# Gate chains spread over more pieces in a fused recurrence and mixture-of-experts kernel

## The chip, the cores and the metric

The kernel runs on one core of a Trainium2 chip. The metric is the device time of one execution in microseconds (us). The core has five engines that run beside each other, each taking its own instructions in order: the tensor engine (PE) for matrix products, the vector engine (DVE), the scalar engine (ACT), GpSimd (POOL) and SyncE (SP), of which the last here only starts transfers. Engines wait for each other through semaphores. Transfers between device memory and the on-chip memory (SBUF) are issued by SP, ACT and POOL and carried out by 16 DMA engines. Matrix products land in PSUM, a small second memory.

## What is computed

Two layers over x of 4 batches, 1024 time steps and 1024 channels, in 32-bit floats:

```python
x = x + ffn0(cond0(x, f, f, w0, u0, cond))       # f is the side input
x = x + ffn1(cond1(x, f, f, w1, u1, cond))

def cond(r, k, v, w, u, time_emb):
    tf = sigmoid(sum(time_emb))
    decay = exp(-exp(w)) * (0.5 + 0.5 * tf)
    ek = exp(min(k, 30)); ekv = ek * v
    # forward and backward over time: a = a * decay + ekv, b = b * decay + ek
    num = nf + nb - ekv + exp(min(u + k, 30)) * v
    den = df + db - ek + exp(min(u + k, 30))
    return sigmoid(r) * num / max(den, 1e-8) * (0.8 + 0.2 * tf)

def ffn0(c): return einsum(c, weight * scale) + bias

def ffn1(c):
    h = rmsnorm(c) * norm_w
    w, ids = top_4(softmax(h @ router_w.T)); w = w / sum(w)
    routed = sum over the 4 of w * ((silu(h @ w1g[id]) * (h @ w1u[id])) @ w2[id])
    shared = (silu(h @ sg) * (h @ su)) @ sd
    return c + routed + shared
```

All of cond apart from sigmoid(r) depends on f alone, so it can be worked out for both layers before x of the second layer is known. The second layer's sigmoid(x), called the gate here, is multiplied in later.

## The kernel before

**Two phases.** The first phase, up to about 2,100 us, makes everything but the experts: the recurrences, the first product, gate, norm, router and the shared feed-forward. The second phase takes 68 pairs of expert blocks and 12 single ones and is the same in both kernels. The change lies in the first phase alone.

**The mixer** (`mixing`, L232) works out the recurrences in units (batch, tile of 128 channels, layer), on DVE (scans L278 and L290, products L308 to L322), ACT (exponentials, logarithm, sigmoid) and with one accumulating DMA of POOL (L323). Each finished unit goes to device memory (c0_d for the first layer, c1_d for the second; L338) and is loaded back in chunks of 512 time steps. It is a generator: each `yield` gives the DVE time that the step was reckoned to take. For the first batch all eight units of the first layer come before those of the second.

**Pieces.** The work of PE is cut into pieces, mostly eight matrix products of 128x512 that end in one PSUM tile, reckoned at 6.9 us (`W_PIECE`). `order` (L850) lists them and `run` goes through the list. For each piece `run` first calls `early` (the loads) of this piece and of the two after it, then draws mixer steps as long as the reckoned DVE work is below the reckoned PE work, then issues the piece. `mix_until` draws mixer steps without that limit until a unit is made. The follow-up of a piece is put off with `after(n, f)`: f is issued at the end of the piece n places later. All this settles only the order of the instructions in each engine's queue, fixed when the kernel is built; at run time each engine goes as far as its semaphores allow.

**Chunks.** The 4096 tokens are eight chunks of 512 (q, two for each batch). The pieces that the change touches:

- `first_ffn(q, gated)`: the first layer's product, eight pieces (L429). With `gated` (chunks 2 to 7) the residual sum x follows (L434), and then the gate of the tile. For chunks 0 and 1 the gates come later.
- `gate(q, ot, x)`: sigmoid on ACT one piece later, on DVE the product with c1 (L458) and on ACT its square (L459) two pieces later, and three pieces later an accumulating DMA on POOL (L462) and a matrix product of ones with the square (L465), by which the squares of all channels are summed in the PSUM tile `ss`. After the eighth of these the norm begins.
- `late_gate(q)`: the gates of chunks 0 and 1 as eight pieces with little PE work. Each loads c1 and x (L482, L484) in `early`, so two pieces ahead, and waits for the c1 unit there with `mix_until`.
- `norm_route(q)`: a generator that `run` steps once a piece: square root on ACT, reciprocal (L499) and scaling (L502) on DVE, router product (L509) on PE, its copy on ACT (L511), then transposes (L520, L528), top four (L531 to L536), ranks, and 16 scattering DMAs on POOL (L591). After chunk 7 it goes on to `plan` (lists of tokens for each expert) and `first_weights` (loads of the first two units of the second phase, L788 and L795).
- `shared_up(q)`: 16 pieces (L620), in turn the gate and the up product of 128 columns; Silu on ACT a piece after the former, the product of both on DVE (L629) a piece after the latter, or at once for the last. `shared_down(q)`: eight pieces (L648), the sum with the residual (L662), and a turn by PE and ACT (L653, L654).

In `order` the first batch is: `first_ffn(0)`, `first_ffn(1)`, the gates of chunk 0, seven empty pieces, then `shared_up(0)` with a gate of chunk 1 after each second piece, the remaining gates, `shared_down(0)`, `shared_up(1)`, `shared_down(1)`. PSUM tiles of these products (`mm`) have four buffers, sigmoid and square (`y`, `sq`, pool `pch`) two each, x six.

Of the kernel before, what the change touches and what calls it, by code (L numbers as in the profile page):

```python
# [8 lines left out]
FP = mybir.dt.float32  # L9
I32 = mybir.dt.int32  # L10
U32 = mybir.dt.uint32
AF = mybir.ActivationFunctionType
ALU = mybir.AluOpType
# [9 lines left out]
P = 128  # L23
CH = 512
# [7 lines left out]
def kernel(  # L32
# [15 lines left out]
    nc = tc.nc  # L48
# [6 lines left out]
    NC = C // P  # L55
    NI = I // P
    NSI = SI // P
# [25 lines left out]
    ones = const.tile([P, P], FP, name="ones")  # L83
# [106 lines left out]
    def right(name, bufs):  # L190
        return a.enter_context(tc.tile_pool(name=name, bufs=bufs, side="right"))
# [8 lines left out]
    px = right("px", 6)  # L200
    pw0 = right("pw0", 3)
    pch = right("pch", 2)
    psm = right("psm", 1)
    ps_ss = a.enter_context(tc.tile_pool(name="ps_ss", bufs=1, space=PSUM))
    ps_sm = a.enter_context(tc.tile_pool(name="ps_sm", bufs=1, space=PSUM))
# [3 lines left out]
    W_PIECE, W_SMALL = 6.9, 1.0  # L209
# [9 lines left out]
    def other(to, of, func, **kw):  # L219
        table[0] = func  # L220
        nc.scalar.activation(to, of, func, **kw)
# [139 lines left out]
    def after(pieces, f, vector=0.0, tensor=0.0):  # L361

        told[0] += 1
        due.append((count[0] + 1 + pieces, told[0], f, vector, tensor))
# [35 lines left out]
    def first_ffn(q, gated):  # L400

        b, cols = q // NCH, bass.ts(q % NCH, CH)
        c0s, tiles, xs = [], {}, {}

        def early(ot):
            if not gated:

                nc.sync.dma_start(out=resT_d[ot, :, bass.ts(q, CH)], in_=xT[b, bass.ts(ot, P), cols])
            else:
                xs[ot] = px.tile([P, CH], FP, name="x")  # L410
                nc.sync.dma_start(out=xs[ot], in_=xT[b, bass.ts(ot, P), cols])
            if ot == 0:
                mix_until(*((b, ct, 0) for ct in range(NC)))
                if q == 0:
                    work["tensor"] += LATENCY
                for ct in range(NC):
                    c0s.append(pc0.tile([P, CH], FP, name="c0"))
                    nc.sync.dma_start(out=c0s[ct], in_=c0_d[b, ct, :, cols])
            tiles[ot] = pw0.tile([P, NC, P], FP, name="w0t")
            nc.sync.dma_start(out=tiles[ot], in_=w0[ot])  # L420
            if gated:
                mix_until((b, ot, 1))
                c1s[q, ot] = (ph, pc1)[q % NCH].tile([P, CH], FP, name="c1")
                nc.sync.dma_start(out=c1s[q, ot], in_=c1_d[b, ot, :, cols])

        def do(ot):
            mm = ps_mm.tile([P, CH], FP, name="mm")
            for it in range(NC):
                nc.tensor.matmul(mm, lhsT=tiles[ot][:, it, :], rhs=c0s[it], start=(it == 0), stop=(it == NC - 1))  # L429
            to = resT_d[ot, :, bass.ts(q, CH)]  # L430
            scale = v["s0"][:, ot : ot + 1]
            if gated:
                x = xs.pop(ot)
                after(1, lambda: nc.vector.scalar_tensor_tensor(x, mm, scale, x, ALU.mult, ALU.add), W_HALF)  # L434
                after(2, lambda: nc.sync.dma_start(out=to, in_=x))
                gate(q, ot, x)
            else:
                y = px.tile([P, CH], FP, name="x")
                after(1, lambda: nc.scalar.activation(y, mm, AF.Copy, scale=scale))
                after(2, lambda: nc.gpsimd.dma_start(out=to, in_=y, accum_op=ALU.add))  # L440

        return [Piece(lambda ot=ot: do(ot), lambda ot=ot: early(ot)) for ot in range(NC)]

    sums = {}

    def gate(q, ot, x):

        b = q // NCH
        c1 = c1s[q, ot]
        held = {}  # L450

        def sigmoid():
            held["y"] = pch.tile([P, CH], FP, name="y")
            other(held["y"], x, AF.Sigmoid, bias=v["b0"][:, ot : ot + 1])

        def gated():
            held["sq"] = pch.tile([P, CH], FP, name="sq")
            nc.vector.scalar_tensor_tensor(c1, c1, nosc[:, b : b + 1], held["y"], ALU.mult, ALU.mult)  # L458
            nc.scalar.activation(held["sq"], c1, AF.Square)  # L459

        def add():
            nc.gpsimd.dma_start(out=resT_d[ot, :, bass.ts(q, CH)], in_=c1, accum_op=ALU.add)  # L462
            if ot == 0:
                sums[q] = ps_ss.tile([P, CH], FP, name="ss")
            nc.tensor.matmul(sums[q], lhsT=ones, rhs=held["sq"], start=(ot == 0), stop=(ot == NC - 1))  # L465
            if ot == NC - 1:
                beside.append(norm_route(q))

        after(1, sigmoid)
        after(2, gated, W_HALF)  # L470
        after(3, add, 0.0, W_SMALL)

    def late_gate(q):


        b, cols = q // NCH, bass.ts(q % NCH, CH)
        xs = {}

        def early(ot):
            mix_until((b, ot, 1))  # L480
            c1s[q, ot] = (ph, pc1)[q % NCH].tile([P, CH], FP, name="c1")
            nc.sync.dma_start(out=c1s[q, ot], in_=c1_d[b, ot, :, cols])  # L482
            xs[ot] = px.tile([P, CH], FP, name="x")
            nc.sync.dma_start(out=xs[ot], in_=resT_d[ot, :, bass.ts(q, CH)])  # L484

        return [
            Piece(lambda ot=ot: gate(q, ot, xs.pop(ot)), lambda ot=ot: early(ot), tensor=W_SMALL)
            for ot in range(NC)
        ]

    scattered = []
# [1 line left out]
    def norm_route(q):  # L493
# [2 lines left out]
        hs = [c1s[q, ct] for ct in range(NC)]  # L496
        rs = p1.tile([P, CH], FP, name="rs")
        other(rs, sums.pop(q), AF.Sqrt, bias=eps_c, scale=1.0 / C)
        nc.vector.reciprocal(rs, rs)  # L499
        yield 3.4, 0.0  # L500
        for ct in range(NC):
# [106 lines left out]
    def shared_up(q):  # L608
        wts = {}

        def early(f, n):
            wts[f, n] = pw.tile([P, NC, P], FP, name="wpc")
            nc.sync.dma_start(
                out=wts[f, n], in_=(sg, su)[n][:, bass.ts(f, P)].rearrange("(k p) f -> p k f", p=P)
            )

        def do(f, n):
            mm = ps_mm.tile([P, CH], FP, name="mm")
            for kt in range(NC):
                nc.tensor.matmul(  # L620
                    mm, lhsT=wts[f, n][:, kt, :], rhs=c1s[q, kt], start=(kt == 0), stop=(kt == NC - 1)
                )
            if n == 0:
                act = acts[q, f] = pa.tile([P, CH], FP, name="sact")
                after(1, lambda: other(act, mm, AF.Silu))
            else:
                act = acts[q, f]

                after(int(f + 1 < NSI), lambda: nc.vector.tensor_tensor(act, act, mm, ALU.mult), W_HALF)  # L629

        return [
            Piece(lambda f=f, n=n: do(f, n), lambda f=f, n=n: early(f, n)) for f in range(NSI) for n in range(2)
        ]
# [143 lines left out]
    def load(unit, at):  # L777

        kind, n = unit
        e = nc.values_load(  # L780
            have["experts"][0:1, kind, n : n + 1],
            engines=[SP],
            min_val=0,
            max_val=E - 1,
            skip_runtime_bounds_check_because="worked out above from counts, and held to that range",
        )
        for k in range(2):
            nc.sync.dma_start(  # L788
                out=have["w1"][at][k],
                in_=w1[bass.ds(e, 1), k * NK * P : (k + 1) * NK * P].rearrange("e (k p) f -> p (e k) f", p=P),  # L790
            )
            if k == 0:
                yield
        yield
        nc.sync.dma_start(  # L795
            out=have["w2"][at], in_=w2[bass.ds(e, 1)].rearrange("e (k p) f -> p (e k) f", p=P)
        )
        yield
# [51 lines left out]
    def order():  # L850

        pieces = first_ffn(0, False) + first_ffn(1, False) + late_gate(0)

        pieces += [Piece(lambda: None, tensor=2.0) for _ in range(7)]
        up, gates = shared_up(0), late_gate(1)
        for i, piece in enumerate(up):
            pieces.append(piece)
            if i % 2 == 1:
                pieces.append(gates.pop(0))
        pieces += gates  # L860
        pieces += shared_down(0) + shared_up(1) + shared_down(1)
        pieces += first_ffn(2, True) + first_ffn(3, True) + shared_up(2) + shared_down(2) + shared_up(3)
        for b in range(2, B):
            q = NCH * b
            pieces += first_ffn(q, True) + first_ffn(q + 1, True) + shared_down(q - 1)
            pieces += shared_up(q) + shared_down(q)
            if b + 1 < B:
                pieces += shared_up(q + 1)
        return pieces
# [476 lines left out]
```

## Time and profile before

| | |
|---|---|
| median of 3 runs | 5193.74 us (5193.41 to 5196.67) |
| the profiled execution | 5197.78 us, its span 5195.8 us |
| PE busy | 4884.7 us, 94% |
| DVE busy | 3129.8 us, 60% |
| ACT busy | 1433.3 us, 28% |
| POOL busy | 764.6 us, 15% |
| granted clock of PE over the span | 0.989 |
| mean over DMA | 205 GB/s |
| 400 to 500 us: PE, DVE, ACT busy | 84.9, 84.7, 75.2 us |
| 600 to 700 us: PE, DVE, ACT busy | 99.8, 87.8, 67.5 us |
| 1500 to 1800 us: PE, DVE busy | 299.1, 28.7 us |

All views are of one execution, with times from the start of the span. A row of the timeline has its start, its time on the engine, engine, line, operation, result and sources, and in brackets the idle time of the engine before it and what ended that. A product of 32-bit floats stands in the trace as two records, so eight products are x16. Line numbers are those of the kernel before.

### The profile page before, as it was taken

To read this page: it belongs to the slowest core of one execution; us is meant where nothing else is said; L and a number is where in the kernel's file an instruction comes from. 1 tells how busy PE (TensorE), PEld (TensorE's weight loads), DVE (VectorE), ACT (ScalarE), POOL (GpSimd) and SP (SyncE) were. 2 spreads that over 40 slices of the span, in tenths; PEclk is the share of its full clock that TensorE was granted. 3 is DMA by queue.
4 is the path that set the end of the run, shared out by engine and by line. 5 is a ranking of instruction groups with operands and counts; after the bars stand their busy time and mean duration, and the time that the engine had idled before them with its cause. 6 is when DMAs were issued, how large, how long until landed. Compare 5 with 4: busy or idle time off the path is not lost.

```text
span 5195.8 us, 36650 instructions
## 1 busy us (share of the span) xinstructions
PE 4884.7 (94%) x13004; PEld 2258.9 (43%) x13004; DVE 3129.8 (60%) x3280; ACT 1433.3 (28%) x1830; POOL 764.6 (15%) x716
## 2 busy tenths in 40 slices
PE   0478999999999999899999999999999999999999
PEld 0233444444444444444444444444444444444444
DVE  9988898899700221556565656565656556665621
ACT  5557566667500120111111111111111111111110
POOL 0113201300210020111111111111111111111110
PEclk9989999999999999999999999999999999999999
DMA  4676669568733754567777677767676777767684
GB/s 137 201 206 174 170 199 266 162 188 254 206 96 101 214 158 152 196 217 239 216 233 231 222 231 226 231 214 238 211 247 207 242 228 220 234 215 242 216 234 122
DMA packets 517155, 1064.92 MB, mean 205 GB/s; under 512 B 29857, under 2 KB 259362, under 8 KB 516354
## 3 DMA queue, kind: packets, MB, share of 16 engines
q1 hardware_dynamic: 386338, 744.70, 42.4%
q0 software_dynamic: 67600, 210.28, 19.2%
q10 hardware_dynamic: 63024, 107.50, 5.9%
q8 instruction: 105, 1.72, 0.1%
q14 instruction: 88, 0.72, 0.0%
HBM read 844.13 MB, written 203.56 MB: 202 GB/s over the span
## 4 chain that ended last, share of the span: by engine, by line
PE 59%; ACT 0%; DMA 0%; issue 0%; DVE 0%; POOLq 0%; ACTq 0%
PE gA L1072 14%; PE gB L1072 9%; PE gC L1072 9%; PE dA L1072 7%; PE dB L1072 5%; PE dC L1072 4%; PE tr L926 2%; PE gA L960 2%; PE gB L960 2%; PE tr L1009 1%; PE dA L1022 1%; PE dB L1022 1%; PE gC L1257 0%; PE gB L1257 0%; PE dA L1257 0%; PE gA L1257 0%
## 5 line engine op out<-in xcount | busy, mean ns | idle before, releaser
L620 PE MATMUL mm<-c,wpc 128*128 128x512 f32 x1792 | 782.7, 597 | 0.0
L429 PE MATMUL mm<-c,w0t 128*128 128x512 f32 x1024 | 451.6, 597 | 199.7 <-DMA w0t<-in_w 199.7
L620 PEld LDWEIGHTS mm<-c,wpc 128*128 128x128 f32 x1792 | 341.4, 192 | 421.0 <-issue 419.4
L1072 PE MATMUL gA<-w,hsT 128*128 128x512 f32 x1088 | 491.4, 594 | 0.0
L1072 PE MATMUL gB<-t_up,s_up 128*128 128x512 f32 x1088 | 489.1, 592 | 0.0
L1072 PE MATMUL gC<-w,s_up 128*128 128x512 f32 x1088 | 489.1, 592 | 0.0
L1056 POOL DMA_INDIRECT sum_d<-y,tokens x148 | 304.7, 2059 | 919.8 <-DMA sum_d<-y,tokens 541.4
L648 PE MATMUL mm<-sact,wpc 128*128 128x512 f32 x896 | 399.4, 601 | 10.9 <-DVE sact L629 10.9
L911 POOL DMA_INDIRECT hs<-h_d,tokens x148 | 149.6, 1011 | 1635.5 <-PE tr L926 1546.2
L429 PEld LDWEIGHTS mm<-c,w0t 128*128 128x128 f32 x1024 | 195.3, 192 | 446.8 <-issue 437.7
L1072 PEld LDWEIGHTS gC<-w,s_up 128*128 128x128 f32 x1088 | 206.7, 190 | 260.2 <-issue 260.2
L1072 PEld LDWEIGHTS gB<-t_up,s_up 128*128 128x128 f32 x1088 | 206.7, 190 | 260.2 <-issue 244.2
L807 DVE TENSOR_TENSOR t_up<-w,w 128x2048 f32<-128x2048 f32 x136 | 310.7, 2285 | 0.0
L1072 PEld LDWEIGHTS gA<-w,hsT 128*128 128x128 f32 x1088 | 202.3, 191 | 229.1 <-issue 229.1
L290 DVE TENSOR_TENSOR_SCAN fg<-decay,tail,fg 128x1024 f32<-128x1024 f32 x128 | 292.9, 2329 | 0.0
L648 PEld LDWEIGHTS mm<-sact,wpc 128*128 128x128 f32 x896 | 169.4, 193 | 212.4 <-issue 198.5
L1072 PE MATMUL dB<-t_down,s_down 128*128 128x512 f32 x544 | 256.9, 594 | 0.1
L1072 PE MATMUL dA<-w,actT 128*128 128x512 f32 x544 | 255.8, 592 | 0.0
L1072 PE MATMUL dC<-w,s_down 128*128 128x512 f32 x544 | 255.8, 592 | 0.0
L927 ACT COPY hsT<-tr 128x512 f32<-128x512 f32 x296 | 172.7, 588 | 293.3 <-PE tr L926 293.3
L1072 PE MATMUL gA<-t_up,hsT 128*128 128x512 f32 x544 | 244.5, 592 | 0.0
L997 ACT ACTIVATE act<-c 128x512 f32<-128x512 f32 x68 | 42.9, 630 | 708.9 <-DVE c L993 708.9
(238 smaller groups left out, 6211.1 us busy)
## 6 DMA issues: line engine op xcount, KB each, us to landing
w<-in_w SPq DMA_DIRECT2D x240, 2048.0 KB, 9.0
fg<-euk POOLq DMA_DIRECT2D x64, 512.0 KB, 6.3
c_d<-r ACTq DMA_DIRECT2D x64, 512.0 KB, 7.9
c<-c_d SPq DMA_DIRECT2D x128, 256.0 KB, 6.3
w0t<-in_w SPq DMA_DIRECT2D x64, 512.0 KB, 5.9
wpc<-in_sg SPq DMA_DIRECT2D x56, 512.0 KB, 4.0
wpc<-in_su SPq DMA_DIRECT2D x56, 512.0 KB, 3.7
wpc<-in_sd SPq DMA_DIRECT2D x56, 512.0 KB, 5.1
```

Of the source, the lines that this page charges most:

```text
L290: nc.vector.tensor_tensor_scan(fg[:, m, ::-1], decay[L][:, ct, b : b + 1].to_broadcast([P, T]), fg[:, m, ::-1], tail[:, m : m + 1], ALU.mu ...
L429: nc.tensor.matmul(mm, lhsT=tiles[ot][:, it, :], rhs=c0s[it], start=(it == 0), stop=(it == NC - 1))
L620: nc.tensor.matmul(mm, lhsT=wts[f, n][:, kt, :], rhs=c1s[q, kt], start=(kt == 0), stop=(kt == NC - 1))
L648: nc.tensor.matmul(mm, lhsT=wts[ct][:, f, :], rhs=acts[q, f], start=(f == 0), stop=(f == NSI - 1))
L807: nc.vector.tensor_tensor(to, x, y, ALU.subtract)
L911: nc.gpsimd.indirect_dma_start(out=hs, out_offset=None, in_=h_d, in_offset=bass.IndirectOffsetOnAxis(ap=tokens[:, i, self.n : self.n + 1], ...
L926: nc.tensor.transpose(tr[:, r, :], hs[:, bass.ts(4 * q + r, P)], ident)
L927: nc.scalar.copy(self.hsT[:, 4 * q : 4 * q + 4, b, :], tr)
L960: nc.tensor.matmul(ps, lhsT=self.hsT[:, k, 0, :], rhs=w[k // NK][:, k % NK, bass.ts(n, I)], start=(k == 0), stop=(k == NC - 1),)
L1022: nc.tensor.matmul(ps, lhsT=self.actT[:, k, 0, :], rhs=w[:, k, bass.ts(n, 512)], start=(k == 0), stop=(k == NI - 1),)
L1056: nc.gpsimd.indirect_dma_start(out=sum_d, out_offset=bass.IndirectOffsetOnAxis(ap=tokens[:, i, self.n : self.n + 1], axis=0), in_=y, in_of ...
L1072: nc.tensor.matmul(ps, lhsT=x[:, k, :], rhs=w[:, k, :], start=(k == 0 and not more), stop=(k == half - 1), skip_group_check=more,)
```

## The change

The sigmoid's result y gets a pool of its own with four buffers, and the square is written over y. The sum waits one piece longer after the gate's product. With `gated` the whole chain starts a piece later (lag 2). The late gates wait for one unit ahead only, and load within the piece before; a piece that only loads the first comes ahead of them. The norm has one more step between square root and reciprocal. The product with the up part comes two pieces later, not one. Around the last gate of chunk 0 the reckoned PE times of the empty pieces change: one of 4.0 before it, seven of 0.5 behind it instead of 2.0 (LATENCY is 12.0).

```diff
@@ pools
     pch = right("pch", 2)
+    psq = right("psq", 4)
@@ first_ffn
-                gate(q, ot, x)
+                gate(q, ot, x, 2)
@@ gate
-    def gate(q, ot, x):
+    def gate(q, ot, x, lag=1):
...
         def sigmoid():
-            held["y"] = pch.tile([P, CH], FP, name="y")
+            held["y"] = psq.tile([P, CH], FP, name="y")
             other(held["y"], x, AF.Sigmoid, bias=v["b0"][:, ot : ot + 1])
 
         def gated():
-            held["sq"] = pch.tile([P, CH], FP, name="sq")
             nc.vector.scalar_tensor_tensor(c1, c1, nosc[:, b : b + 1], held["y"], ALU.mult, ALU.mult)
-            nc.scalar.activation(held["sq"], c1, AF.Square)
+            nc.scalar.activation(held["y"], c1, AF.Square)
...
-            nc.tensor.matmul(sums[q], lhsT=ones, rhs=held["sq"], start=(ot == 0), stop=(ot == NC - 1))
+            nc.tensor.matmul(sums[q], lhsT=ones, rhs=held["y"], start=(ot == 0), stop=(ot == NC - 1))
...
-        after(1, sigmoid)
-        after(2, gated, W_HALF)
-        after(3, add, 0.0, W_SMALL)
+        after(lag, sigmoid)
+        after(lag + 1, gated, W_HALF)
+        after(lag + 3, add, 0.0, W_SMALL)
@@ late_gate
-        def early(ot):
+        def load(ot):
             mix_until((b, ot, 1))
...
-        return [
-            Piece(lambda ot=ot: gate(q, ot, xs.pop(ot)), lambda ot=ot: early(ot), tensor=W_SMALL)
-            for ot in range(NC)
+        def do(ot):
+            if ot + 1 < NC:
+                load(ot + 1)
+            gate(q, ot, xs.pop(ot))
+
+        return [Piece(lambda: None, lambda: load(0), tensor=0.0)] + [
+            Piece(lambda ot=ot: do(ot), tensor=W_SMALL) for ot in range(NC)
         ]
@@ norm_route
         other(rs, sums.pop(q), AF.Sqrt, bias=eps_c, scale=1.0 / C)
+        yield 0.0, 0.0
         nc.vector.reciprocal(rs, rs)
@@ shared_up
-                after(int(f + 1 < NSI), lambda: nc.vector.tensor_tensor(act, act, mm, ALU.mult), W_HALF)
+                after(2 if f + 1 < NSI else 0, lambda: nc.vector.tensor_tensor(act, act, mm, ALU.mult), W_HALF)
@@ order
         pieces = first_ffn(0, False) + first_ffn(1, False) + late_gate(0)
 
-        pieces += [Piece(lambda: None, tensor=2.0) for _ in range(7)]
+        pieces.insert(-1, Piece(lambda: None, tensor=LATENCY / 3))
+        pieces += [Piece(lambda: None, tensor=0.5) for _ in range(7)]
         up, gates = shared_up(0), late_gate(1)
```

## The prediction

> **What bounds the kernel now.** I read the busy rows first, then what the tensor engine (PE) waited for, its timeline at those waits, and what the vector engine (DVE) waited for at the same moments.
>
> The page's slices: busy tenths, 130 us each.
>
> ```profile
> PE   0478999999999999899999999999999999999999
> DVE  9988898899700221556565656565656556665621
> ```
>
> PE is the bound from 197 us on; DVE is nearly as full until about 1,430 us, while the mixer (the scans) runs. Busy PE is 4884.7 of 5195.8 us, so 311 us are idle. Who was waited for (total, times, longest):
>
> ```profile
> PE mm L429 <- DMA w0t<-in_w: 199.7, 5, 197.2
> PE ss L465 <- ACT sq L459: 54.9, 12, 16.1
> PE mm L648 <- DVE sact L629: 10.9, 2, 9.0
> PE tr L926 <- DMA hs<-h_d,tokens: 10.8, 1, 10.8
> PE tr L520 <- ACT rT L654: 8.5, 6, 7.3
> PE tr L509 <- DVE c L502: 5.0, 1, 5.0
> ```
>
> The first row is the mixer's lead-in, which the change doesn't touch. The target is the second: the one-column-sum matmul that closes each gate (L465) stands in PE's queue before sigmoid, gate and square are through. PE's timeline there (start, us, what, idle before):
>
> ```profile
> 336.89 2.08 PE L465 MATMUL ss<-sq,ones 128*128 128x512 f32 x2 [16.08 <-ACT sq L459]
> ...
> 358.88 8.60 PE L509 MATMUL tr<-c,rw_sb 128*32 128x512 f32 x16 [5.04 <-DVE c L502]
> ...
> 369.45 7.03 PE L620 MATMUL mm<-c,wpc 128*128 128x512 f32 x16
> ...
> 407.67 2.07 PE L465 MATMUL ss<-sq,ones 128*128 128x512 f32 x2 [6.46 <-ACT sq L459]
> 409.54 15.76 PE L620 MATMUL mm<-c,wpc 128*128 128x512 f32 x32
> 425.13 1.02 PE L465 MATMUL ss<-sq,ones 128*128 128x512 f32 x2
> 425.99 13.90 PE L620 MATMUL mm<-c,wpc 128*128 128x512 f32 x32
> ```
>
> A stall costs more than its idle time: after 6.46 us of it the same two blocks took 2.07 and 15.76 us, against 1.02 and 13.90 without one. And DVE's waits in the same stretch:
>
> ```profile
> 389.53 1.23 DVE L256 TENSOR_TENSOR ekv<-ek,k 128x1024 f32<-128x1024 f32 x1 [5.14 <-ACT ek L217]
> ...
> 433.01 1.23 DVE L314 TENSOR_TENSOR r<-r,fg 128x1024 f32<-128x1024 f32 x1 [3.92 <-DMA fg<-euk]
> ...
> 511.99 0.69 DVE L629 TENSOR_TENSOR sact<-sact,mm 128x512 f32<-128x512 f32 x1 [6.49 <-PE mm L620]
> ...
> 1055.99 0.69 DVE L629 TENSOR_TENSOR sact<-sact,mm 128x512 f32<-128x512 f32 x1 [8.09 <-ACT sact L221]
> ```
>
> So the engines wait for each other in turn. DVE executes in order: what it loses, every later gate loses.
>
> **The change part by part.** The operations and their number stay, but for one more table load on ScalarE (ACT). What moves is seen in the order of each engine's instructions, built from both kernels.
>
> *Gates of the first chunk (313 to 359 us).* Only the next unit is awaited before a gate is issued, so on DVE gate 4 comes before the 11.6 us of mixer work (330.04 less 318.48) instead of behind it, and the pair L321/L322 (2.4 us) moves ahead of the norm's reciprocal. Followed row by row: DVE keeps the mixer work up to there; ACT gets gate 4's square and gate 5's sigmoid between two mixer steps and switches tables twice more before the exponential, so the last c1 unit is written later: 2 x 1.28 us, with the sigmoid and square some 2.8 us after overlap. Before, its load went out at 337.6 and its sigmoid ran at 346.0, so most of that delay lies beside other work: sigmoid at 347.5, gate 8 at 348.3 (before: 350.26), reciprocal at 352.5 (354.60). Gain **2.1**, and 0.7 because a matmul block now fills the wait of L528: **2.8**.
>
> Here a rule speaks against the change. The Trainium skill ("ScalarE: Activation LUTs", What ACT_TABLE_LOAD costs) puts a switch at 1283 ns and a drain of about 1380 ns, 2.66 us together, and advises grouping functions by table set; the change splits the groups. The row has the load alone: it starts at 310.97 for 1.28 us, and the sigmoid follows at 312.26. By the page two switches would cost 5.3 us and turn 2.1 into a loss of 0.7; by the row, 2.6. I take the row.
>
> *Gates of the second chunk (372 to 545 us).* Their closing matmul moves from three pieces behind the gate to four, and the gates themselves one up-pair later, because the list of gates now begins with a piece that only loads: the first sum stands behind the seventh up piece, before it was the fourth. That is 20.6 us more cover (3 x 6.87). The four stalls (6.46, 5.02, 3.63, 5.17: 20.3) and the slow blocks after them (4 x 1.05, and 1.86, 2.01, 0.62, 0.87: 9.6) could all go: **29.9**. But DVE must keep up. Its L531 (logits out of PSUM) ran at 370.07 unhindered; now PE has up piece, L509, up piece (8.6 + 6.9 + 6.9) before it issues L528, so DVE, done at about 365.6, waits until 379.6: **14 us new**, with all the gates behind it.
>
> *Four buffers y, the square written into y.* Same space (y and sq had two each). It removes ACT's waits for PE at the square (51.6 us, eight times), which cost nothing themselves.
>
> *The product with the up matmul (L629) two pieces later.* DVE's waits for PE there (6.49, 1.32) go. What it costs: the PSUM tile is held a piece longer, with four of them. Before, the product ended 7.2 to 8.6 us ahead of the next user in the tightest place (1,014 and 1,026 us); a piece later, 0.3 to 1.7 us are left. Between 0 and some 7 us; hidden if DVE gains about what PE gains. Taken as 0.
>
> *Gated chunks (two pieces more to the sum).* Stalls of 1.52, 3.94 and 2.17 us go, with 1.8 us of slow blocks: 7.2 before 1,056 us, 2.2 after; with the wait for w0t of 0.75 at 1,284 us, which followed the stall, about **3** after.
>
> *Up to down (sact).* PE waits 1.88 (720 us) and 8.99 (1,048 us), with 2.5 us of slow matmuls after the second. In the new order the third block's last Silu no longer stands behind a mixer exponential that waited 3.79 us for a DMA.
>
> *The end of the stage (2,046 to 2,112 us).* Sum and reciprocal come three pieces later (lag 1, sum 1, the added yield 1), so plan, token lists and the first expert weights do too: SyncE's queue has the first load behind the fifth down piece instead of the second, 3 x 7.3 = 22 us. The second half of the first unit's w1 still goes where the fourth load went, 2,076; landing takes up to 13.1 us, so 2,090, and its user starts at 2,096: hidden, with 6 us of cover. What can't be hidden: three 2 MB loads now run beside the first token gather, for which PE waits 10.8 us. It took 5.8 us; gathers took 3.9 to 10.2. From 0 to 4.4, and I take **3**.
>
> **The sum.** At 1,056 us there are two accounts. PE, if nothing is ever late: 2.8 + 29.9 + 1.9 + 11.5 + 7.2 = 53. DVE: 6.5 less mixer work issued by then (seven empty pieces of 2.0 become 0.5 each plus one of 4.0), the waits of 5.14, 4.29 and 3.92 (the third follows from the second; POOL's slot writes blocked that DMA for 13 us, now for about 4), 6.49, 1.32 and 8.09 (29.2), and half of three whose order changes (8.7 at the reciprocal, 9.2 at 719 us, 6.2 at a sigmoid: 12); less 14 and about 7 for L531 in the second chunk: 27. The later engine decides, so 27, not 53. With 3 after it and 3 lost at the end: **27 us**. The profiled execution took 5197.78 (span 5195.8), 4 above the median; the difference goes onto the median: 5193.74 - 27 = **5167**.
>
> **The rivals.**
> 1. *DVE's arrears eat it* (chance 0.16): the stalls leave L465 and come back at L629, L509 or as a PSUM wait, and only the 6.5 us of postponed mixer work stay. For: DVE is 89% busy from 600 to 1,200 us. Against: much of its idle time is waiting for PE and ACT. Time 5187.
> 2. *DVE becomes slower than before* (0.12): L531, behind one more PE piece in each norm, waits 14 us in the first and up to 7 in the next three while the mixer runs: 35. If none of the removed waits stays away, 35 - 6.5 = 28 and more than it can hide; with a third of them gone, 5193.7 + 28 - 10 = 5212. It decides from new waits above 6.5 plus what the removed ones give. Against: L531 waited only 1.7 us in the second norm, where pieces already lay between.
> 3. *All of the cover works* (0.14): DVE's own waits go with PE's, two thirds of PE's account: 35 + 3 + 8 for the tr wait at 587 us (7.28) and its slow blocks, nothing lost at the end: 5148.
> That the gates don't move is excluded by the order.
>
> **How the numbers follow.** Forecast 0.58, the rivals 0.16, 0.12 and 0.14. A measurement here can't tell less than 0.2% (10 us) from no change. Faster: 0.58 + 0.14 and a little of the first rival: 0.75; within: 0.14; slower: 0.11. The forecast's own range is 5155 to 5180 (the L629 and gather ends, and the halved waits lost or won); to leave out no more than 2 in 10 it reaches to 5148 and 5190.
>
> **What would show it.** Right: L465 under 15 us in PE's waits, a wait of 10 to 15 us at DVE's L531 near 380 us, the first up matmul at about 357 us, the PE row near 1,048 us less than 3 us idle, the end of the last down piece near 2,067 us. Wrong: PE waiting for L629 at an up matmul, L509 waiting for L502 near 557 us, or a gather above 8 us at the end.

## The result and the profile after

The changed kernel took **5170.45 us** (median of five runs, 5167.34 to 5180.32) against 5195.63 (5193.41 to 5196.67): a ratio of 0.9957 with a 95% interval of 0.9943 to 0.9972, 25 us faster. The profiled execution took 5180.32 us (span 5178.3), the longest of the five, so its views show less of a gain than the median.

Who PE waited for (total, times, longest), changed kernel:

```profile
PE mm L430 <- DMA w0t<-in_w: 202.5, 7, 197.0
PE ss L465 <- ACT y L459: 42.2, 8, 17.2
PE tr L932 <- DMA hs<-h_d,tokens: 17.8, 2, 17.0
...
PE mm L653 <- DVE sact L634: 3.7, 1, 3.7
```

The sums' row fell from 54.9 us only to 42.2, the row from up to down (L629 before, L634 now) from 10.9 to 3.7; the wait at the first token gather grew from 10.8 to 17.8. PE's timeline, changed kernel:

```profile
342.22 2.07 PE L465 MATMUL ss<-y,ones 128*128 128x512 f32 x2 [17.24 <-ACT y L459]
...
358.68 9.45 PE L625 MATMUL mm<-c,wpc 128*128 128x512 f32 x16 [5.00 <-issue]
368.06 7.05 PE L514 MATMUL tr<-c,rw_sb 128*32 128x512 f32 x16
...
444.87 1.66 PE L465 MATMUL ss<-y,ones 128*128 128x512 f32 x2 [4.58 <-ACT y L459]
...
466.62 2.08 PE L465 MATMUL ss<-y,ones 128*128 128x512 f32 x2 [5.20 <-ACT y L459]
...
511.50 2.07 PE L465 MATMUL ss<-y,ones 128*128 128x512 f32 x2 [4.73 <-ACT y L459]
```

In the new order the first up piece goes ahead of the router product (L514), and of the four stalls of the second chunk three are left, 14.5 of 20.3 us. DVE in the same stretch shows the price that was forecast, the wait for the logits (L536), and two waits behind a transfer that landed late:

```profile
382.58 0.29 DVE L536 COPY lg<-small 128x128 f32<-128x128 f32 x1 [14.98 <-PE small L533]
...
443.22 1.23 DVE L315 TENSOR_TENSOR r<-r,fg 128x1024 f32<-128x1024 f32 x1 [4.00 <-DMA fg<-euk]
449.13 1.23 DVE L257 TENSOR_TENSOR ekv<-ek,k 128x1024 f32<-128x1024 f32 x1 [4.68 <-ACT ek L218]
```

Where the gain sits, from the start of the same piece in both timelines (shift against before, us): first down piece of chunk 0 +0.8 (512.6 to 513.4); that of chunk 1 -4.1; first piece of chunk 2 -7.2; first up piece of chunk 3 -19.6 (1110.9 to 1091.3); end of the last down stage -22.2 (2097.0 to 2074.8); first turn of gathered tokens -16.0 (2107.8 to 2091.8).

A second profile of the same kernel (below) belongs to an execution of 5166.32 us. There the shifts are -10.2, -15.2, -18.7, -30.8, -34.6 and -28.7. The median lies between the two.

### The profile page after: what moved, and what is told of

Its sections match the earlier page's. It is cut to its first block, busy times and chain, and to the rows that moved or that the text cites. A ratio compares the mean times of both kernels' runs of the same rounds, so it can differ in the third digit from the quotient of the medians.

```text
span 5178.3 us, 36602 instructions
## 1 busy us (share of the span) xinstructions
PE 4875.7 (94%) x13004; PEld 2256.4 (44%) x13004; DVE 3130.4 (60%) x3280; ACT 1435.0 (28%) x1831; POOL 762.3 (15%) x716
## 4 chain that ended last, share of the span: by engine, by line
PE 87%; DVE 5%; DMA 4%; ACT 3%; issue 2%; POOL 0%; SPq 0%; ACTq 0%; DVEq 0%; POOLq 0%
PE gA L1078 14%; PE mm L625 12%; PE gC L1078 9%; PE gB L1078 9%; PE dA L1078 7%; PE mm L430 7%; PE mm L653 6%; PE dB L1078 5%; PE dC L1078 5%; PE tr L932 2%; PE gA L966 2%; PE gB L966 2%; PE tr L1015 1%; DMA xg<-in_xT 1%; PE tr L514 1%
```

## The experiments

| kernel | median us | ratio to before (95%) |
|---|---|---|
| changed kernel again | 5172.33 | 0.9956 (0.9943 to 0.9970) |
| without the norm's added step | 5188.53 | 0.9988 (0.9979 to 0.9997) |
| old empty pieces | 5186.38 | 0.9985 (0.9976 to 0.9994) |
| sum two pieces behind, not three | 5171.95 | 0.9955 (0.9942 to 0.9969) |
| product with up one piece later | 5173.06 | 0.9951 (0.9937 to 0.9965) |
| lag 1 for chunks 2 to 7 | 5174.04 | 0.9962 (0.9948 to 0.9975) |
| old loading of late gates | 5167.93 | 0.9946 (0.9932 to 0.9959) |
| before, with the later sum alone | 5190.50 | 0.9992 (0.9984 to 1.0001) |
| nine empty pieces | 5164.45 | 0.9936 (0.9923 to 0.9950) |
| last norm three pieces earlier | 5171.88 | 0.9953 (0.9940 to 0.9967) |
| these two together | 5157.73 | 0.9929 (0.9915 to 0.9942) |
| and the old loading | 5154.99 | 0.9923 (0.9909 to 0.9936) |

**1. The changed kernel again**, no edit.

> The changed kernel once more. In its first profile an accumulating transfer of the mixer (fg<-euk, issued at 426.65 us) landed only at 443.1 us and made the vector engine and ScalarE wait some 8 us; in the profile of the kernel with the earlier last norm, which has the same instructions there, it was issued at 425.75 us and nothing waited for it. Theory X (this one landing decides between two courses of the first batch): a profile with the early landing has the first down piece of chunk 0 at about 502 us instead of 513.5 and a span of about 5168 us; the median stays at 5168 to 5172. Rival: the profile is like the first, and the 5 to 10 us between executions come from elsewhere (the end).

The first down piece of chunk 0 began at 502.4 us, as theory X has it, and the span was 5164.3 us (about 5168 was said; the median of 5172.33 lies at the upper edge of what was said). PE's waits in this stretch:

```profile
457.04 1.12 PE L465 MATMUL ss<-y,ones 128*128 128x512 f32 x2 [0.88 <-ACT y L459]
...
500.57 2.07 PE L465 MATMUL ss<-y,ones 128*128 128x512 f32 x2 [6.23 <-ACT y L459]
```

One kernel so has stalls of 14.5 or 7.1 us here, depending, as far as the two profiles show, on when one transfer lands (last section). The experiments that follow are compared by their medians, and their profiles with this second one.

**2. Without the norm's added step.**

```diff
-        yield 0.0, 0.0
         nc.vector.reciprocal(rs, rs)
```

> The changed kernel without the added step between square root and reciprocal in the norm. Theory N (the step is the room that a later sum needs: with the sum alone a piece later, PE waited 15.1 us at router products and the vector engine 41.7 us for square roots): both waits come back in part in chunks 1 to 3, the vector engine's wait for square roots before 1430 us rises by 8 us or more over the changed kernel's, time 2 to 6 us above it, although the first norm's logits come one up piece earlier (about 7 us less wait there). Rival: that first norm decides, and the time is 3 to 6 us below the changed kernel, as with nine empty pieces.

Theory N, with more than it asked for: 16 to 18 us slower, two thirds of the whole gain, from one step that adds no instruction. (The profiled execution, 5183.92 us, was the fastest of its eleven.) Of DVE's waits from 340 to 1,430 us, the rows for the square root (total, times, longest; kernel without the step):

```profile
DVE rs L503 <- ACT rs L222: 30.3, 5, 10.9
...
DVE rs L503 <- issue: 10.3, 1, 10.3
```

Before the change the row read 33.8 in six waits; with the step it is 5.6 and 2.1 (first profile) or 8.0 (second). PE's waits at the router product, none with the step, came back with 5.8 us. How it reaches PE is seen in chunk 1's norm, DVE's timeline of the kernel without the step:

```profile
547.78 3.35 DVE L503 RECIPROCAL rs<-rs 128x512 f32<-128x512 f32 x1 [6.86 <-ACT rs L222]
...
555.97 0.74 DVE L666 SCALAR_TENSOR_TENSOR rT<-mm,v_b,rT 128x512 f32<-128x512 f32 x1
```

and PE's:

```profile
556.86 1.09 PE L657 MATMUL tr<-ident,rT 128*128 128x128 f32 x4 [6.58 <-DVE rT L666]
```

The reciprocal stands at the head of DVE's queue and waits for ACT's square root. PE had ended the last sum at 535.7 us, but ACT began the root only at 547.06: in ACT's queue two transfers to issue, four activations of the mixer, a copy and three table loads of 1.28 us stood ahead of it. Behind the reciprocal stand four mixer operations and the residual sum of a down piece, and PE, which turns that sum, waits 6.58 us. With the step, DVE does those four and that residual sum first, and the reciprocal at 545.38 (second profile) waits 0.82 us; ACT's root is no earlier after its sum there (533.9 to 544.66).

**3. Old empty pieces.**

```diff
-        pieces.insert(-1, Piece(lambda: None, tensor=LATENCY / 3))
-        pieces += [Piece(lambda: None, tensor=0.5) for _ in range(7)]
+        pieces += [Piece(lambda: None, tensor=2.0) for _ in range(7)]
```

> The changed kernel with the old empty pieces (seven reckoned at 2.0 us behind the last gate, none of 4.0 before it). Theory M (mixer work before the first norm costs what it lasts): up to 6.5 us more of the vector engine's mixer steps stand ahead of the reciprocal of chunk 0, its first router product waits for the scaled tiles 4 us or more longer, time 3 to 7 us above the changed kernel. Rival: the vector engine waits there for ScalarE anyway, and the mixer's steps fill that wait; time within 2 us.

Theory M, again with more than it asked for: 14 to 16 us slower. DVE's timeline of this kernel:

```profile
354.35 2.28 DVE L279 TENSOR_TENSOR_SCAN fg<-decay,ek 128x1024 f32<-128x1024 f32 x1
356.55 2.27 DVE L279 TENSOR_TENSOR_SCAN fg<-decay,ekv 128x1024 f32<-128x1024 f32 x1
359.94 3.35 DVE L504 RECIPROCAL rs<-rs 128x512 f32<-128x512 f32 x1 [1.12 <-ACT rs L222]
```

Two scans stand ahead of the reciprocal, which began 5.5 us earlier in the changed kernel (354.44). That they stand earlier in DVE's order lasts through the first phase, for each mixer step is placed against the same reckoned sum. PE's further waits in this profile:

```profile
364.18 8.86 PE L625 MATMUL mm<-c,wpc 128*128 128x512 f32 x16 [9.35 <-issue]
...
889.36 5.67 PE L625 MATMUL mm<-c,wpc 128*128 128x512 f32 x8 [5.25 <-DVE c L507]
...
1264.46 9.27 PE L430 MATMUL mm<-c,w0t 128*128 128x512 f32 x16 [8.44 <-DMA w0t<-in_w]
```

The mixer itself was not late (its last scans began at 1348.9 us against 1347.4 in the second profile and 1374.9 in the kernel before), while the reciprocal of chunk 5 came at 1392.3 instead of 1373.0. Work was not added; it stood before work that PE waits for.

**4. The sum two pieces behind again.**

```diff
-        after(lag + 3, add, 0.0, W_SMALL)
+        after(lag + 2, add, 0.0, W_SMALL)
```

> The changed kernel with the sum of squares two pieces behind the gate's product again instead of three, everything else as changed. Theory C (cover still counts once the other parts are in): each sum in the second chunk stands a piece of 6.9 us nearer to its gate, the stalls after 372 us rise from 7 to 15 us to 20 or more, time 4 to 9 us above the changed kernel. Rival D: the vector engine's course is the same and PE only waits at another place; time within 3 us.

Rival D: no difference. The second chunk's stalls were 11.1 us, inside what one kernel shows from execution to execution.

**5. The product with up one piece later.**

```diff
-                after(2 if f + 1 < NSI else 0, lambda: ...
+                after(int(f + 1 < NSI), lambda: ...
```

> The changed kernel with the product behind the up matmul one piece later again instead of two. Theory D: the vector engine waits for PE at this product again, 6 us or more in total before 545 us, and the time is 2 to 6 us above the changed kernel, about 5174 us. Rival: the second piece only holds the PSUM tile longer; then PE's waits don't grow, and the time is the same or up to 4 us lower.

Theory D missed: DVE's waits for PE at this product before 545 us didn't return (2.6 us, for ACT, in both), and the ratio is that of the changed kernel. Later they did grow, for ACT's Silu: up to the mixer's last scan 29.5 us in all against 13.1 in the second profile, without a loss in time that shows. Why the waits for PE were there before was not tried.

**6. Lag 1 for chunks 2 to 7.**

```diff
-                gate(q, ot, x, 2)
+                gate(q, ot, x)
```

> The changed kernel with the gates of chunks 2 to 7 starting one piece after their product again, not two (the sum is still three pieces behind that). Theory C: stalls of 1 to 4 us come back at the sums of chunks 2 and 4, 2 to 5 us in total, and the time is 2 to 5 us above the changed kernel. Rival: the later sum alone covers them; the norms come a piece earlier and the time is the same or up to 3 us lower.

Inconclusive: 0.0006 above in the ratio, 2 to 4 us by the medians. PE's 5.5 us at the sums of this kernel were waits for the square root, which has to read `ss` (one buffer) before the next chunk's first sum, not for the squares.

**7. Old loading of the late gates** (two pieces ahead, no loading piece).

```diff
-        def load(ot):
+        def early(ot):
...
+        return [
+            Piece(lambda ot=ot: gate(q, ot, xs.pop(ot)), lambda ot=ot: early(ot), tensor=W_SMALL)
...
```

> The changed kernel with the old loading in the late gates (two pieces ahead, waiting for two more units, no piece that only loads). Theory C (cover counts: PE pieces between a gate's product and its sum): the second chunk's first sum stands two up pieces earlier, the stalls there rise from 14.5 us to 20 or more, and gate 4 of the first chunk stands behind 11 us of mixer work again; time 6 to 14 us above the changed kernel, about 5180 us. Rival D only (the vector engine's own waits decide, and the place of a sum doesn't change these): time within 4 us of the changed kernel.

Theory C missed, with its sign: not slower, and stalls of 3.1 us in the second chunk. The gates stand two up pieces earlier here, on DVE too. The first reciprocal began at 352.9 us instead of 354.4, but 1.5 us of that lie ahead of the gates: ACT's table load before the first sigmoid began at 311.17 us here and at 312.66 in the changed kernel, where ACT had waited 1.56 us for a transfer of the mixer.

**8. The later sum alone, on the kernel before** (four buffers, the square over y).

```diff
-        after(3, add, 0.0, W_SMALL)
+        after(4, add, 0.0, W_SMALL)
```

> The kernel before with one part of the change alone: the sigmoid's result in a pool of four buffers, the square written over it, and the sum of squares one piece later, for all chunks. Theory C (cover of the sums is the main part): stalls at the sums after 372 us fall from 27.9 us in total to under 14, time 10 to 18 us below the kernel before. Rival D (the vector engine decides; its order is nearly unchanged here, so that what PE doesn't wait for at the sums it waits for at sact or at the first weights): less than 7 us below the kernel before.

Rival D: 4 us, not clear of nothing. The cover works where it is (stalls after 372 us in the second chunk 7.1 instead of 20.3; first down piece 9.0 us earlier), but PE then waits for the norm. Waits of PE, this kernel:

```profile
PE ss L465 <- ACT y L459: 37.4, 10, 16.2
PE tr L509 <- DVE c L502: 15.1, 3, 9.4
...
PE ss L465 <- ACT rs L222: 5.1, 2, 2.6
```

DVE, whose order hasn't changed, waits 41.7 us for the square roots. It is not always the sum that makes the root late: in chunk 3 the last sum ended at 929.9 us (before: 939.1), and the root began at 944.1 (939.9), behind, among others, a mixer sigmoid in ACT's queue that waited 4.39 us for its load. What helped here was to move the reciprocal (run 2), not the sum.

**9. Nine empty pieces** instead of seven, so that the router product and the logits' turn stand ahead of the first up piece again.

```diff
+        pieces += [Piece(lambda: None, tensor=0.0) for _ in range(2)]
```

> The changed kernel with nine empty pieces instead of seven behind chunk 0's last gate (the two more are reckoned at 0), so that the first norm's router product and the transposes of its logits stand ahead of the first up piece again. Theory D (the vector engine decides until the mixer ends, and its new wait of 15.0 us at the logits' copy near 383 us kept the stalls at the second chunk's sums): that wait falls under 2 us, PE's waits for the squares between 400 and 545 us fall from 14.5 to under 6 us, time 8 to 14 us below the changed kernel, so about 5160 us. Rival P (the wait of the vector engine is slack, PE has what it can get): the wait falls as well, but comes back at another instruction of the vector engine in the same stretch, and the time stays within 4 us of the changed kernel's 5170.

Near theory D: 6 to 8 us faster by the medians (8 to 14 was said), DVE's wait 5.39 us at 368.55 (not under 2), the second chunk's stalls 5.4. All five runs (5159.57 to 5165.07) lie below all ten of the changed kernel (from 5166.32), though the intervals of the ratios overlap.

**10. The last norm three pieces earlier.**

```diff
-                gate(q, ot, x, 2)
+                gate(q, ot, x, 1 if q == NT // CH - 1 and ot > 3 else 2)
...
-        after(lag + 3, add, 0.0, W_SMALL)
+        after(lag + (2 if q == NT // CH - 1 and ot > 3 else 3), add, 0.0, W_SMALL)
...
-        yield 0.0, 0.0
+        if q != NT // CH - 1:
+            yield 0.0, 0.0
```

> The changed kernel with the last chunk's second four gates at the old distances (lag 1, sum two pieces behind the product) and without the added step in the norm of that chunk, so that its norm, the plan and the first expert weights come three pieces earlier. Theory E (the end gives 5 to 7 us back because SyncE's three loads of 2 MB are bunched behind the last down piece and run beside the first token gather): PE's wait at the gather falls from 17.0 us to under 11.5, time 4 to 7 us below the changed kernel, about 5165 us. Rival: the gather's wait has nothing to do with the loads' places (it is the way from the last write-out to the gather): the wait stays over 14 us and the time within 2 us of 5170.

The wait fell to 10.4 us as theory E has it, but the median didn't move. The first batch's two courses, 11 us apart, may cover a gain of this size in five runs; the profiled execution, which had the early landing, spans 5159.5 us against the 5164.3 of run 1. Hence the same edit on nine empty pieces:

> The changed kernel with both nine empty pieces and the last chunk's norm three pieces earlier. Theory E: PE's wait at the first gather falls from 17 us to about 10.5, and the time is 3 to 7 us below that of the nine empty pieces alone (ratio to before about 0.9925). Rival (what the earlier norm wins at the gather it loses at the last chunk's own sums, as PE's 3.8 us of wait in the last down stage suggest): the ratio stays within 0.0006 of 0.9936.

Here 5156.73 to 5160.14 us against 5159.57 to 5165.07, and a wait of 10.5 us against 17.1. The wait is shown as theory E has it; the gain is 4 us by the ratios, which lie 0.0007 apart where the rival allowed 0.0006, and 7 by the medians, so its size is not settled.

**11. The edits of 7, 9 and 10 together.**

> Nine empty pieces, the last chunk's norm three pieces earlier, and the old loading of the late gates, all on the changed kernel. If the old loading is worth something of its own (its kernel had a ratio of 0.9946 beside 0.9956 and 0.9957), the ratio to before is 0.9915 to 0.9922, about 5153 us. Rival (it wins at the same place as the empty pieces): 0.9926 to 0.9933, as the other two alone.

5154.99 us (5150.09 to 5156.82), the fastest of all. Its end, PE's timeline:

```profile
2054.94 0.63 PE L655 MATMUL tr<-ident,rT 128*128 128x128 f32 x4 [2.48 <-DVE rT L664]
2066.09 1.94 PE L930 MATMUL tr<-ident,hs 128*128 128x128 f32 x8 [10.52 <-DMA hs<-h_d,tokens]
```

and of the changed kernel (first profile):

```profile
2074.20 0.63 PE L658 MATMUL tr<-ident,rT 128*128 128x128 f32 x4 [1.58 <-DVE rT L667]
2091.78 1.94 PE L932 MATMUL tr<-ident,hs 128*128 128x128 f32 x8 [16.96 <-DMA hs<-h_d,tokens]
```

The ratio, 0.9923, lies between the two expectations: whether the old loading adds 3 us or nothing can't be told.

## Why the prediction was right, and where its terms were not

**The sum held by stages, its composition did not.** Predicted 27 us, measured 25. In the two profiles PE stood 19.6 and 30.8 us earlier at the first up piece of chunk 3 (27 forecast at 1,056 us), gained 2.6 and 3.8 from there to the end of the last down stage (3 forecast) and lost 6.2 and 5.9 at the first gather (3 forecast). That the parts within the 27 came out otherwise and still made up the sum is in part luck.

The account by DVE is what the runs show. From 340 us to the start of the mixer's last scans (1374.9 us before, 1359.2 and 1347.4 in the two profiles after) DVE worked 905, 904 and 903 us and was idle 130, 115 and 104: the mixer ends earlier by what DVE no longer waits. PE's cover alone buys little: the later sum alone is worth 4 us, and of the four edits that lengthen chains or move loads each could be taken back without a loss that can be measured. (Whether all four could at once wasn't tried.) But when the mixer ends is not all that counts. With the old empty pieces it ended 26 us earlier than before, and PE's last turn came only 14 us earlier (2082.1 against 2096.4): which work DVE does first counts too.

**First chunk (2.8 us): mis-sized.** The reciprocal was forecast at 352.5 and began at 354.44; the gain of 2.1 was 0.2. The two extra table loads took 1.28 us each, with the next activation 1.29 us after the load's start (328.83 to 330.12), so the row was right and not the 2.66 of the Trainium skill ("ScalarE: Activation LUTs", What ACT_TABLE_LOAD costs). But ACT had waited 1.56 us for a transfer of the mixer before the first sigmoid, which began 1.7 us later than before (312.26 to 313.95); the mixer's own ACT steps moved 3 us back with DVE's, and the last sigmoid, forecast at 347.5, came at 349.77. In the profile with the old loading, where that transfer was in time, the reciprocal began at 352.9. The first up matmul was forecast at 357 and came at 358.68.

**The wait at the logits (14 us): right,** 14.98 and 14.53 us. Stalls of 7.1 and 14.5 us stayed in the second chunk; with the wait at 5.39 us (run 9) they were 5.4.

**The product behind the up matmul:** DVE's waits for PE went and no PSUM wait came, both as said; but the time is the same without the second piece (run 5).

**Gated chunks:** the three stalls went (7.6 us), but waits for w0t grew from 2.5 us to 5.5 (first rows of the two lists, less the lead-in). **Up to down:** 1.88 to 0, 8.99 to 3.68; less than 3 was said.

**The step that was mis-sized is DVE's account at 1,056 us.** DVE's waits from 340 to 1,430 us, before:

```profile
DVE sact L629 <- ACT sact L221: 34.0, 7, 9.2
DVE rs L499 <- ACT rs L221: 33.8, 6, 10.4
...
DVE sact L629 <- PE mm L620: 13.1, 3, 6.5
DVE lg L531 <- PE small L528: 12.7, 2, 11.0
```

and in the changed kernel (first profile):

```profile
DVE lg L536 <- PE small L533: 38.0, 4, 21.8
...
DVE sact L634 <- ACT sact L222: 13.7, 4, 6.8
...
DVE rs L504 <- ACT rs L222: 5.6, 3, 3.5
```

The longest waits of the roots and the logits come after the mixer's last scan. Up to it:

| DVE waits at | before | after, two profiles | forecast gain |
|---|---|---|---|
| square roots (rs) | 23.4 us | 4.1, 4.4 | 4.4 |
| the product behind the up matmul (sact) | 47.1 us | 13.7, 13.1 | 20.5 |
| the logits (lg) | 1.7 us | 16.2, 15.6 | -21 |

"Half of three whose order changes ... 12" holds what the norm's added step does, at 4.4 us for the one reciprocal counted; otherwise that step was priced only as a piece of delay at the end. It acts in every norm, and run 2 puts it at 16 to 18 us. The waits at the product shrank by 13 us more than was counted; which edit did that isn't shown. "6.5 less mixer work" was counted at its own duration; run 3 puts it at 14 to 16, since the steps stay earlier in DVE's order through the norms that follow (one profile; which of PE's later waits there, 5.25 and 8.44 us, belong to it wasn't tried by itself). Against these, of the 29.2 us of "removed waits" 15.5 stayed in the first profile (4.00, 4.68 and 6.78 us) and 6.8 in the second: POOL issued the transfer fg<-euk after 3 us of blocking, as forecast (4), but in the first profile it landed late. The parts overlap, so they don't add.

**The end (3 us, 0 to 4.4): too small, with one term left out.** PE's wait was 16.96 and 16.72 us, 6 more than before. The gather itself was slower, which is the term that was counted: from its issue to PE's first use 8.5 and 9.3 us against 6.0. It was also issued later, 8.4 and 7.5 us after PE's last turn against 4.8, and that was put at nothing. In the first profile SyncE's last loads of expert weights stood behind two loads of rT, which waited 10.7 us for buffers still being written out, and POOL's gather began at 2083.25, when one of these weights landed. By pieces of delay over all profiles: none or one 10.4 to 10.8 us, two 13.2 to 15.5, three 16.1 to 17.2.

**The signs.** Near what was said came the wait at the logits and the first up matmul. Missed: the sums' row stayed at 42.2 us, not under 15 (17.24 of it is the first chunk's wait, 16.08 before; the forecast counted only 2.8 us of gain in that chunk); PE's row from up to down was 3.7, not under 3. Of the signs of being wrong one came, a gather above 8 us.

**The rivals:** rival 1 (the gain eaten by DVE's arrears) is nearly what the later sum alone does; rival 2 had its mechanism in the first norm, but in chunks 1 to 3 the logits' wait was under 1 us; rival 3 (all cover works) said 5148, which this kernel did not reach; run 11, another kernel, came to 5155.

## What to carry to other kernels

Where two in-order engines exchange work, look first at what waits at the head of each queue and what stands behind it: taking out the step that moves one instruction behind ready work, and costs nothing, lost 16 to 18 us here, while a longer distance to the consumer, put alone into the kernel before, gained 4 us, not clear of nothing. When a chain gets longer, move everything that consumes its end by as much, and then look at who issues transfers behind it. Price an edit that seems to cost nothing by the waits that it removes in every place where it acts, not only where its delay is seen.

## What the runs showed of the hardware

One accumulating transfer of 512 KB (fg<-euk), issued at nearly the same moment in two executions of one kernel (426.65 and 426.06 us), landed at about 443.1 us in the first and after 5.8 us in the second. (In the kernel without the added step, issued at 426.50, ACT could use it at 436.58.) In the first, ACT waited 6.96 us for it and DVE 4.00, and the first down piece came 11 us later (513.4 and 502.4). That the landing made these 11 us is argued from the waits behind it; nothing was run that moves the landing alone. Why it took three times as long isn't known.
